# Centering and output projection of the product's groups as one matmul per token column on half of the array rows

## The chip, the cores and the metric

The kernel runs on one core of a Trainium2 chip. The metric is the device time of one execution in microseconds; the time of the kernel before is the median of three runs. A profile comes from one further execution, whose own time is given with it.

## The reference, cut to what matters

The input x is a 512 x 512 x 64 image in float32. Two layers follow each other. The first one normalises x by group, takes a layer norm over the 64 channels, makes gated left and right projections, multiplies them as a matrix product per channel over the image's axes, and finishes with a layer norm, a projection and a gate:

```
left  = (xn @ left_w + left_b) * mask * sigmoid(xn @ lgate_w + lgate_b)
right = (xn @ right_w + right_b) * mask * sigmoid(xn @ rgate_w + rgate_b)
out = einsum('bkjd,bkid->bijd', left, right)
out = _ln(out, onorm_w, onorm_b) @ out_w + out_b
x = x + out * sigmoid(xn @ ogate_w + ogate_b)
```

The second layer adds a spectral convolution with 12 x 12 modes of the group-normalised result. The change is in the line with `_ln(out)` and `out_w`: mean and variance of the product over its 64 channels, and the projection.

## The kernel before, in words

The mask leaves about half of the rows and columns, so the product is 256 x 256 tokens of 64 channels (`K` is 256). It is computed channel by channel and lies in SBUF as `places`, 128 partitions by 512 token columns of 64 channels. A *group* is 64 columns, so that there are 8 groups of the product (`first` = 8), followed by 32 units of x, each also 64 columns. One software pipeline runs over all of them (the loop over `s`): a step handles 8 columns, 128 partitions x 512 elements, and a group or a unit takes 8 steps (`SIZE`). The order of instructions is written out by hand (`manual_schedule`); every engine works through its own list in that order.

At step `s` the loop issues, for the groups of the product:

- TensorE transposes the 8 columns of step `s + 13` (`transpose`, L924): four 128 x 128 transposes, each of two columns, so that the channels of the one column lie on partitions 0 to 63 and those of the other on 64 to 127. ScalarE copies the result from PSUM to SBUF as `xt_c` (L927).
- TensorE multiplies the transposed columns of step `s` by `weights["out"]` (`times`, L934), a 128 x 128 matrix with the projection twice on its diagonal; the result is `w_ps`. The layer norm's centering and scale were multiplied into that matrix.
- TensorE multiplies the transposed columns of step `s + 12` by `center` (`centered`, L934), again a matrix of two diagonal blocks; the result `c_ps` is the columns less their means. ScalarE squares it into `sq_c` (L944).
- VectorE sums the squares of two steps over the channels (`summed`, L948), which are those of steps `s + 10` and `s + 11`. Once per group ScalarE takes the root of these sums (L954) and VectorE its reciprocal (L1106).
- VectorE multiplies `w_ps` by the reciprocal roots into `z_t` (L1112), and adds the bias for two steps at once (L1115). SyncE's queue stores `z_t` to DRAM as `u_d` (L1118), 512 KB per two steps.

The steps before 0 are the lead-in: transposes, centering, squares and sums, without `w_ps` and z. The steps of the last 13 before 64 already transpose and center the first units of x, whose matrices are `center_x` and `gate_x`.

Among the units the same steps go on with more work in them: ScalarE takes a sigmoid (L1068), POOL multiplies by rows of u that SyncE's queue loads from `u_d` (`load_u`, L965) or by the bias row (`gated`, L974) and adds to x (`added`, L978), VectorE takes statistics (L1023), and the result is stored. POOL's queue gathers x (`load`, L628). A closing stage, which is mostly transfers, adds the spectral part and writes the output.

An earlier stage, which makes the left and right sides, projects with matmuls on 64 of the 128 array rows: `project` (L746) multiplies `weights[k][h]` for each half `h` of the partitions and writes each half to its own bank of a tile of two banks.

PSUM in this stage: two tiles of one bank for the transposes, two for `c_ps`, two for `w_ps`, one bank for `scratch` (sums and biases), one for `f_ps`; all eight are taken.

Of the kernel before, what the change touches and what calls it, by code (L numbers as in the profile page):

```python
# [9 lines left out]
F32 = mybir.dt.float32  # L10
I32 = mybir.dt.int32
AF = mybir.ActivationFunctionType
ALU = mybir.AluOpType
AX = mybir.AxisListType
PSUM = bass.MemoryType.PSUM
DRAM = bass.MemoryType.DRAM

P = 128
N = 512
C = 64  # L20
# [26 lines left out]
def conv_preact_kernel(ctx: ExitStack, tc: tile.TileContext, t: dict):  # L47
    nc = tc.nc
    x, out = t["x"], t["out"]
# [18 lines left out]
    center = load_const("c_center", [P, P])  # L68
# [13 lines left out]
    with tc.tile_pool(name="ix", bufs=1) as xp, tc.tile_pool(  # L82
        name="ixp", bufs=1, space=PSUM
# [51 lines left out]
    weights, biases = {}, {}  # L135
# [476 lines left out]
    def compact(fc):  # L612
# [31 lines left out]
        with tc.tile_pool(name="xc", bufs=1) as cp:  # L644
            xc = cp.tile([P, K + 1, 2, C], F32, name="xc")
            with tc.tile_pool(name="f1", bufs=1) as sp, tc.tile_pool(name="f1x", bufs=2) as xp, tc.tile_pool(
                name="f1y", bufs=4
# [19 lines left out]
                for jc in range(NJ):  # L667
                    if jc % quarter == 0:
                        stats = sp.tile([P, 1, 16 * quarter, 6], F32, name="stats1c")
                    for r in range(4):  # L670
                        flat = xgs[jc][1][r].rearrange("p j c -> p (j c)")
                        for c in range(4):

                            ps = pt.tile([P, 4, P], F32, name="x_ps")
# [18 lines left out]
            with tc.tile_pool(name="fb", bufs=QB + 8) as gp, tc.tile_pool(name="fw", bufs=2) as wk, tc.tile_pool(  # L693
                name="fr", bufs=3
# [111 lines left out]
        with tc.tile_pool(name="tri", bufs=1) as trp:  # L806
# [50 lines left out]
            SIZE = 8  # L857
# [6 lines left out]
            with tc.manual_schedule(), tc.tile_pool(name="late", bufs=1) as lp:  # L864
# [27 lines left out]

                    (nc.gpsimd if h == 3 else nc.sync).dma_start(modes_t, modes_d[h * P : (h + 1) * P])

                with tc.tile_pool(name="np_x", bufs=LEAD + 2) as tp, tc.tile_pool(name="np_q", bufs=2) as sqp, tc.tile_pool(
                    name="np_s", bufs=3
                ) as small, tc.tile_pool(name="oz", bufs=4) as zp, tc.tile_pool(
                    name="o1", bufs=1
                ) as s1, tc.tile_pool(name="np_t", bufs=2, space=PSUM) as ps_t, tc.tile_pool(
                    name="np_c", bufs=2, space=PSUM  # L900
                ) as ps_c, tc.tile_pool(name="np_w", bufs=2, space=PSUM) as ps_w, tc.tile_pool(
                    name="np_n", bufs=1, space=PSUM
                ) as ps_n, tc.tile_pool(name="opf", bufs=1, space=PSUM) as ps_f:
                    scratch = ps_n.tile([P, 4, P], F32, name="scratch")
                    sum_ps = [scratch[:, 3, i * G : (i + 1) * G] for i in range(2)]
                    bias_ps = {"out": scratch[:, 2, :C], "ogate": scratch[:, 2, C:]}
# [11 lines left out]
                    def transpose(s):  # L918
                        k, n = divmod(s, SIZE)
                        flat = (place(k) if k < first else x_of(k - first)).rearrange("p n c -> p (n c)")  # L920
                        tps = ps_t.tile([P, 4, P], F32, name="t_ps")
                        for i in range(4):
                            o = (8 * n + 2 * i) * C
                            nc.tensor.transpose(tps[:, i, :], flat[:, o : o + P], ident)  # L924
                        xts[s] = tp.tile([P, 4, P], F32, name="xt_c")
                        if k < first:
                            nc.scalar.copy(xts[s], tps)  # L927
                        else:
                            nc.scalar.activation(xts[s], tps, AF.Identity, bias=ab1[:, 2:3])  # L929

                    def times(pool, name, s, w):
                        ps = pool.tile([P, 8, C], F32, name=name)
                        for i in range(4):
                            nc.tensor.matmul(ps[:, 2 * i : 2 * i + 2, :], xts[s][:, i, :], w, start=True, stop=True)  # L934
                        return ps

                    def centered(s):
                        return times(ps_c, "c_ps", s, center if s < first * SIZE else center_x)

                    def squared(s, cps):  # L940
                        n = s % SIZE
                        if n % 2 == 0:
                            sqs[s // 2] = sqp.tile([P, 16, C], F32, name="sq_c")
                        nc.scalar.activation(sqs[s // 2][:, 8 * (n % 2) : 8 * (n % 2) + 8, :], cps, AF.Square)  # L944

                    def summed(s):
                        k, n = divmod(s, SIZE)
# [99 lines left out]
                    for s in range(-LEAD, total_g + 2 * SIZE):  # L1047
# [6 lines left out]
                        if s + LEAD < total_g:  # L1054
                            transpose(s + LEAD)
                        wps = cps = None
                        if 0 <= s < total_g:
                            wps = times(ps_w, "w_ps", s, weights["out"] if k < first else gate_x)
                            del xts[s]
                        if 0 <= s + LEAD - 1 < total_g:  # L1060
                            cps = centered(s + LEAD - 1)
# [280 lines left out]
```

## Time and profile before

| what | value |
|---|---|
| median of 3 runs | 1892.95 us (1892.57 to 1894.03) |
| time of the profiled execution | 1886.98 us |
| its span, first to last instruction | 1885.2 us |
| PE busy in the span | 1683.2 us |
| DVE busy | 1458.5 us |
| ACT busy | 922.0 us |
| POOL busy | 873.0 us |
| first transposes of the product's groups | 666.3 us |
| z of step 0, of step 64 | 686.3 us, 829.1 us |
| end of the units | about 1546 us |

PE is TensorE's matmuls, PEld its weight loads, DVE is VectorE, ACT ScalarE, POOL GpSimd, SP SyncE. A float32 matmul of two operands is two records of the profile (two passes), a transpose is one. A matmul's record is longer than the time by which it moves the next one on, since matmuls are pipelined: what counts is the distance between starts. In a list of groups a line has the line of the kernel, engine, operation, output and inputs, sizes and count, then busy time, mean duration in ns, and the idle time of the engine before it with what ended it. In the waits a line has the waiting engine and tile, the one waited for, and the sum in us, the count and the longest wait.

### The profile page before, as it was taken

To read this page: it belongs to the slowest core of one execution; us is meant where nothing else is said; L and a number is where in the kernel's file an instruction comes from. 1 tells how busy PE (TensorE), PEld (TensorE's weight loads), DVE (VectorE), ACT (ScalarE), POOL (GpSimd) and SP (SyncE) were. 2 spreads that over 40 slices of the span, in tenths; PEclk is the share of its full clock that TensorE was granted. 3 is DMA by queue.
4 is the path that set the end of the run, shared out by engine and by line. 5 is a ranking of instruction groups with operands and counts; after the bars stand their busy time and mean duration, and the time that the engine had idled before them with its cause. 6 is when DMAs were issued, how large, how long until landed. Compare 5 with 4: busy or idle time off the path is not lost. (4 is left out here: it accounts for less than half of the span.)

```text
span 1885.2 us, 33737 instructions
## 1 busy us (share of the span) xinstructions
PE 1683.2 (89%) x11598; PEld 1350.9 (72%) x11598; DVE 1458.5 (77%) x2997; ACT 922.0 (49%) x1606; POOL 873.0 (46%) x678
## 2 busy tenths in 40 slices
PE   6779899998999999999999999999999956998873
PEld 5666666664788889998888888788888835664441
DVE  5989677777555568888999799979999994665552
ACT  3565555653222255567777677757767720111000
POOL 3655111111000000029999799979998982111110
PEclk9989899999999999999999899989999986555555
DMA  6999155556656534237777676767777589999999
GB/s 250 387 373 382 62 141 135 138 140 160 206 179 179 151 137 165 116 136 259 260 235 251 219 238 243 242 219 259 254 262 248 199 226 366 419 427 427 426 427 389
DMA packets 188868, 468.22 MB, mean 248 GB/s; under 512 B 35184, under 2 KB 134384, under 8 KB 147600
## 3 DMA queue, kind: packets, MB, share of 16 engines
q1 hardware_dynamic: 158192, 262.40, 41.4%
q0 software_dynamic: 27856, 202.19, 28.1%
q8 instruction: 94, 1.54, 0.3%
q10 hardware_dynamic: 2640, 1.38, 0.3%
q14 instruction: 86, 0.70, 0.1%
HBM read 278.13 MB, written 187.76 MB: 247 GB/s over the span
## 5 line engine op out<-in xcount | busy, mean ns | idle before, releaser
L934 PE MATMUL w_ps<-gate_x,xt_c 128*128 128x128 f32 x2048 | 281.9, 282 | 32.1 <-DVE z_t L1112 30.7
L978 POOL TENSOR_TENSOR places<-places,z_t 128x1024 f32<-128x1024 f32 x127 | 302.1, 2378 | 8.2
L934 PEld LDWEIGHTS w_ps<-gate_x,xt_c 128*128 128x128 f32 x2048 | 253.1, 195 | 49.1 <-DVE z_t L1112 48.6
L934 PE MATMUL c_ps<-center_x,xt_c 128*128 128x128 f32 x2048 | 276.3, 278 | 0.2
L934 PEld LDWEIGHTS c_ps<-center_x,xt_c 128*128 128x128 f32 x2048 | 252.5, 194 | 2.3 <-ACT xt_c L929 1.1
L944 ACT ACTIVATE sq_c<-c_ps 128x512 f32<-128x512 f32 x320 | 188.6, 590 | 104.3 <-PE c_ps L934 103.8
L1254 PE MATMUL l_ps<-places,rinv 24*128 24x512 f32 x512 | 209.7, 1128 | 31.7 <-DVE places L1261 25.7
L1112 DVE TENSOR_TENSOR z_t<-w_ps,rs_n 128x512 f32<-128x512 f32 x320 | 216.1, 675 | 23.0 <-PE w_ps L934 22.7
L1023 DVE BATCH_NORM_STATS2 stats2c<-places 128x6 f32<-128x128 f32 x1024 | 220.5, 279 | 8.1 <-POOL places L978 8.1
L948 DVE TENSOR_REDUCE scratch<-sq_c 128x16 f32<-128x1024 f32 x160 | 194.6, 1216 | 16.6 <-ACT sq_c L944 11.8
L1068 ACT ACTIVATE z_t<-z_t 128x1024 f32<-128x1024 f32 x128 | 135.5, 1058 | 142.0 <-DVE z_t L1115 117.7
L1115 DVE TENSOR_TENSOR z_t<-z_t,scratch 128x1024 f32<-128x1024 f32 x160 | 195.4, 1221 | 11.7 <-ACT rs_n L954 3.4
L1254 PEld LDWEIGHTS l_ps<-places,rinv 24*128 24x128 f32 x512 | 120.9, 304 | 115.4 <-DVE places L1261 73.1
L974 POOL TENSOR_TENSOR z_t<-z_t,bias_row_out 128x1024 f32<-128x1024 f32 x63 | 149.6, 2374 | 113.0 <-DMA places<-u_d 108.7
L924 PE MATMUL t_ps<-c_ident,places 128*128 128x128 f32 x1280 | 196.6, 277 | 1.3 <-DVE places L853 1.3
L1261 DVE TENSOR_TENSOR places<-places,l_ps 128x512 f32<-128x512 f32 x200 | 124.2, 683 | 86.5 <-DMA places<-x_h,dst_i 53.4
L929 ACT ACTIVATE xt_c<-t_ps,ab_xc 128x512 f32<-128x512 f32 x256 | 175.8, 687 | 23.8 <-PE t_ps L924 23.8
L924 PEld LDWEIGHTS t_ps<-c_ident,places 128*128 128x128 f32 x1280 | 148.9, 143 | 52.3 <-issue 52.3
L628 POOL DMA_INDIRECT places<-in_x,src_i x64 | 62.6, 978 | 261.9 <-PE c_ps L934 210.9
L974 POOL TENSOR_TENSOR z_t<-z_t,places 128x1024 f32<-128x1024 f32 x64 | 151.3, 2365 | 32.2 <-ACT z_t L1068 32.0
L678 DVE BATCH_NORM_STATS2 stats1c<-x_ps 128x6 f32<-128x512 f32 x256 | 156.0, 683 | 12.2 <-PE x_ps L677 11.3
L853 DVE SCALAR_TENSOR_TENSOR places<-tri_c_ps,slot_t,mask_s 128x256 f32<-128x256 f32 x128 | 73.1, 650 | 85.3 <-PE tri_c_ps L849 85.3
(203 smaller groups left out, 2641.9 us busy)
## 6 DMA issues: line engine op xcount, KB each, us to landing
x_h<-places SPq DMA_DIRECT2D x64, 1024.0 KB
out_x<-places SPq DMA_DIRECT2D x50, 1024.0 KB
places<-u_d SPq DMA_DIRECT2D x512, 64.0 KB
left_d<-o_c SPq DMA_DIRECT2D x64, 256.0 KB
right_d<-o_c SPq DMA_DIRECT2D x64, 256.0 KB
left_raw<-left_d SPq DMA_DIRECT2D x64, 256.0 KB
right_raw<-right_d SPq DMA_DIRECT2D x64, 256.0 KB
u_d<-z_t SPq DMA_DIRECT2D x32, 512.0 KB
```

The costliest lines, as they stand in the source:

```text
L678: nc.vector.bn_stats(stats[:, 0, 16 * (jc % quarter) + 4 * r + c, :], ps.rearrange("p i k -> p (i k)"))
L924: nc.tensor.transpose(tps[:, i, :], flat[:, o : o + P], ident)
L929: nc.scalar.activation(xts[s], tps, AF.Identity, bias=ab1[:, 2:3])
L934: nc.tensor.matmul(ps[:, 2 * i : 2 * i + 2, :], xts[s][:, i, :], w, start=True, stop=True)
L944: nc.scalar.activation(sqs[s // 2][:, 8 * (n % 2) : 8 * (n % 2) + 8, :], cps, AF.Square)
L948: nc.vector.tensor_reduce(totals[k % 2][:, 8 * (n - 1) : 8 * (n + 1)], sqs.pop(s // 2), AX.X, ALU.add)
L974: nc.gpsimd.tensor_mul(zs[k, c], zs[k, c], u)
L978: nc.gpsimd.tensor_add(xr, xr, zs.pop((k, c)))
L1023: nc.vector.bn_stats(st[k // 4][:, g, k % 4, :], x_of(k)[:, :, 2 * g : 2 * g + 2])
L1112: nc.vector.tensor_mul(z[:, 8 * odd : 8 * odd + 8, :], wps, rs)
L1115: nc.vector.tensor_add(z, z, bias.unsqueeze(1).to_broadcast([P, 16, C]))
L1254: nc.tensor.matmul(ps.rearrange("p j o -> p (j o)"), rinv[h, b, :], it[h], start=True, stop=True, tile_position=(32 * g, 0),)
```

## The change

For the groups of the product, the two matrices are put side by side: `both` has 64 columns of `center` and 64 columns of `weights["out"]`, once on partitions 0 to 63 and once on 64 to 127. `centered` multiplies the transposed columns by it, one half of the partitions at a time: eight matmuls with 64 rows per step, each for one token column and each 128 output columns wide. The results of the two halves go to the two banks of `y_ps` (two buffers, four banks). ScalarE squares the centered part as before and copies the projected part to SBUF, as the tile `xt_c` (15 buffers); the transposed columns lie in a tile of their own, `xt_y` (two buffers). `w_ps` is no longer computed for the groups: VectorE multiplies the copy by the reciprocal roots. When the pipeline reaches the first unit of x in `centered` (step 52), the pool of `y_ps` is closed and those of `c_ps` and `w_ps` are opened in its place. The units are computed as before.

```diff
--- before.py
+++ after.py
@@ -892,15 +892,24 @@
 
                     (nc.gpsimd if h == 3 else nc.sync).dma_start(modes_t, modes_d[h * P : (h + 1) * P])
 
-                with tc.tile_pool(name="np_x", bufs=LEAD + 2) as tp, tc.tile_pool(name="np_q", bufs=2) as sqp, tc.tile_pool(
+                with tc.tile_pool(name="np_x", bufs=LEAD + 2) as tp, tc.tile_pool(
+                    name="np_y", bufs=2
+                ) as yp, tc.tile_pool(name="np_q", bufs=2) as sqp, tc.tile_pool(
                     name="np_s", bufs=3
                 ) as small, tc.tile_pool(name="oz", bufs=4) as zp, tc.tile_pool(
                     name="o1", bufs=1
                 ) as s1, tc.tile_pool(name="np_t", bufs=2, space=PSUM) as ps_t, tc.tile_pool(
-                    name="np_c", bufs=2, space=PSUM
-                ) as ps_c, tc.tile_pool(name="np_w", bufs=2, space=PSUM) as ps_w, tc.tile_pool(
                     name="np_n", bufs=1, space=PSUM
-                ) as ps_n, tc.tile_pool(name="opf", bufs=1, space=PSUM) as ps_f:
+                ) as ps_n, tc.tile_pool(name="opf", bufs=1, space=PSUM) as ps_f, ExitStack() as products:
+
+                    ps_y = products.enter_context(tc.tile_pool(name="np_b", bufs=2, space=PSUM))
+                    ps_c = ps_w = None
+
+                    both = lp.tile([P, P], F32, name="both")
+                    for h in range(2):
+                        hs = slice(h * C, (h + 1) * C)
+                        nc.vector.tensor_copy(both[hs, :C], center[hs, hs])
+                        nc.vector.tensor_copy(both[hs, C:], weights["out"][hs, hs])
                     scratch = ps_n.tile([P, 4, P], F32, name="scratch")
                     sum_ps = [scratch[:, 3, i * G : (i + 1) * G] for i in range(2)]
                     bias_ps = {"out": scratch[:, 2, :C], "ogate": scratch[:, 2, C:]}
@@ -922,7 +931,7 @@
                         for i in range(4):
                             o = (8 * n + 2 * i) * C
                             nc.tensor.transpose(tps[:, i, :], flat[:, o : o + P], ident)
-                        xts[s] = tp.tile([P, 4, P], F32, name="xt_c")
+                        xts[s] = (yp if k < first else tp).tile([P, 4, P], F32, name="xt_y" if k < first else "xt_c")
                         if k < first:
                             nc.scalar.copy(xts[s], tps)
                         else:
@@ -935,13 +944,32 @@
                         return ps
 
                     def centered(s):
-                        return times(ps_c, "c_ps", s, center if s < first * SIZE else center_x)
+                        if s >= first * SIZE:
+                            return times(ps_c, "c_ps", s, center_x)
+
+                        ps = ps_y.tile([P, 2, 4, P], F32, name="y_ps")
+                        for i in range(4):
+                            for h in range(2):
+                                hs = slice(h * C, (h + 1) * C)
+                                nc.tensor.matmul(ps[:, h, i, :], xts[s][hs, i, :], both[hs], start=True, stop=True)
+
+                        xts[s] = tp.tile([P, 4, P], F32, name="xt_c")
+                        return ps
+
+                    def raw(s):
+                        return xts[s].rearrange("p i (h c) -> p (i h) c", h=2)
 
                     def squared(s, cps):
                         n = s % SIZE
                         if n % 2 == 0:
                             sqs[s // 2] = sqp.tile([P, 16, C], F32, name="sq_c")
-                        nc.scalar.activation(sqs[s // 2][:, 8 * (n % 2) : 8 * (n % 2) + 8, :], cps, AF.Square)
+                        sq = sqs[s // 2][:, 8 * (n % 2) : 8 * (n % 2) + 8, :]
+                        if s >= first * SIZE:
+                            nc.scalar.activation(sq, cps, AF.Square)
+                        else:
+                            by_half = lambda t: t.rearrange("p (i h) c -> p h i c", h=2)
+                            nc.scalar.activation(by_half(sq), cps[:, :, :, :C], AF.Square)
+                            nc.scalar.copy(by_half(raw(s)), cps[:, :, :, C:])
 
                     def summed(s):
                         k, n = divmod(s, SIZE)
@@ -1054,8 +1082,12 @@
                         if s + LEAD < total_g:
                             transpose(s + LEAD)
                         wps = cps = None
+                        if s + LEAD - 1 == first * SIZE:
+                            products.close()
+                            ps_c = products.enter_context(tc.tile_pool(name="np_c", bufs=2, space=PSUM))
+                            ps_w = products.enter_context(tc.tile_pool(name="np_w", bufs=2, space=PSUM))
                         if 0 <= s < total_g:
-                            wps = times(ps_w, "w_ps", s, weights["out"] if k < first else gate_x)
+                            wps = raw(s) if k < first else times(ps_w, "w_ps", s, gate_x)
                             del xts[s]
                         if 0 <= s + LEAD - 1 < total_g:
                             cps = centered(s + LEAD - 1)
```

## The prediction

> **What bounds the stage now.** I read the page's slices first, then the busy time by stretch, the waits inside the stretch, the order of time, and at last the older stage that already works on half the array rows. The product's groups run from about 666 us (first transposes) over step 0 at 686 us to step 64 at 829 us. Busy time by stretch (us of PE, PEld, DVE, ACT, POOL; then clock, DMA share, GB/s):
>
> ```profile
> 667.00:684.00 17.00, 15.97 (x142) 15.51 (x140) 6.07 (x6) 14.01 (x26) 2.92 (x3) 1.00 0.42 133
> 732.00:748.00 16.00, 16.00 (x146) 16.00 (x145) 13.62 (x16) 8.03 (x16) 0.00 (x0) 1.00 0.28 113
> 860.00:880.00 20.00, 18.22 (x158) 16.09 (x157) 19.49 (x45) 14.96 (x23) 19.60 (x9) 1.00 0.73 237
> ```
>
> In the steps (second line) TensorE never pauses and its clock is whole; DVE has 15% to spare, ACT half, DMA is at 28%. Later, among the units (third line), POOL and DVE are full instead. The waits between 690 and 826 us say the same: everyone waits for PE.
>
> ```profile
> ACT sq_c L944 <- PE c_ps L934: 67.3, 61, 1.2
> DVE z_t L1112 <- PE w_ps L934: 13.2, 23, 0.6
> ```
>
> In order of time (start, duration, engine, line), one step and a half:
>
> ```profile
> 739.05 1.23 DVE L948 TENSOR_REDUCE scratch<-sq_c 128x16 f32<-128x1024 f32 x1
> 739.92 0.60 PE L924 MATMUL t_ps<-c_ident,places 128*128 128x128 f32 x4
> 740.12 0.60 ACT L944 ACTIVATE sq_c<-c_ps 128x512 f32<-128x512 f32 x1 [1.15 <-PE c_ps L934]
> 740.18 0.68 DVE L1112 TENSOR_TENSOR z_t<-w_ps,rs_n 128x512 f32<-128x512 f32 x1
> 740.35 1.06 PE L934 MATMUL w_ps<-w_out,xt_c 128*128 128x128 f32 x8
> 740.61 0.58 ACT L927 COPY xt_c<-t_ps 128x512 f32<-128x512 f32 x1
> 741.25 1.06 PE L934 MATMUL c_ps<-c_center,xt_c 128*128 128x128 f32 x8
> 741.45 0.69 DVE L1112 TENSOR_TENSOR z_t<-w_ps,rs_n 128x512 f32<-128x512 f32 x1 [0.58 <-PE w_ps L934]
> 742.14 0.60 PE L924 MATMUL t_ps<-c_ident,places 128*128 128x128 f32 x4
> 742.17 1.22 DVE L1115 TENSOR_TENSOR z_t<-z_t,scratch 128x1024 f32<-128x1024 f32 x1
> 743.50 1.23 DVE L948 TENSOR_REDUCE scratch<-sq_c 128x16 f32<-128x1024 f32 x1
> ```
>
> Transposes follow each other every 742.14 - 739.92 = 2.22 us: 0.43 for four transposes, 0.90 for the eight passes of w_ps, 0.89 for those of c_ps (a float32 matmul is two records), that is 20 passes at 0.111. This is the period of a step, and PE sets it. (z at 829.12 less z at 686.30) / 64 = 2.23 agrees.
>
> The channel stage earlier shows two matmuls on 64 rows each, writing different halves of a two-bank tile:
>
> ```profile
> 350.06 0.19 PEld L746 LDWEIGHTS gates_c<-xnc,w_gates 64*128 64x128 f32 x2 [0.24 <-issue]
> 350.49 1.02 PE L746 MATMUL gates_c<-xnc,w_gates 64*128 64x512 f32 x4
> 351.45 0.66 PE L738 MATMUL rc_ps<-c_ident,rbc 128*128 128x128 f32 x4
> 352.38 1.06 PE L715 MATMUL cc_ps<-c_center,gc_t 128*128 128x128 f32 x8
> 353.36 1.13 PE L746 MATMUL sides_c<-xnc,w_sides 64*128 64x512 f32 x4
> L746 PE MATMUL gates_c<-xnc,w_gates x256: 589/589/693, 227.7 to 462.6; 64*128 64x512 f32 x128
> ```
>
> Four passes of 589 ns each (last line: min/median/max) fit in 1.02 us, so they ran two by two: 0.43 a pair. The two weight loads fit in 0.19, the length of one (182 to 187 ns), so loads of the two halves coincide as well.
>
> **What the Trainium skill says.** (1) TensorE: Matmul & The Clock Gate, "Part 3: Packing small matmuls — row/col tiling": matmuls and weight loads on different row groups run side by side. The gates' lines agree. (2) TensorEngine Tiling (Array Packing), "Key Properties": a change of tiling mode drains the array. The trace agrees. Into halves: cc_ps at 352.38 plus 8 x 0.111 hands over at 353.27; the first record of sides_c stands at 353.36 but is 693 instead of 589 ns long, so its stream began 0.10 later, at 353.46: 0.19 lost. Back: two pairs of gates_c end at 350.49 + 0.86 = 351.35, and the four transposes from 351.45 take 0.49 up to the next ones at 351.94 instead of 0.44: the stream began at 351.50, 0.15 lost. (3) The same page, "PSUM Bottleneck": tiling speeds up TensorE, not the emptying of PSUM. Here ACT gets one more copy for it. (4) VectorE: DVE Perf Modes, "Mode 2×_2P — use both read ports for one tensor": a float32 tensor_tensor stays at one element per cycle. In this trace a 128x512 reduction out of SBUF took 678 ns (L777) and z out of PSUM 675 (L1112), so z gains nothing by reading SBUF.
>
> **The change, part by part.** Steps 0 to 63 are meant, with a lead-in of 13 steps; squares run 12 steps ahead of z.
>
> 1. Removed: the four w_ps matmuls (8 passes) of each of the 64 steps, and the four c_ps matmuls on all rows, of which 64 steps too.
> 2. Added on PE: eight matmuls on 64 rows per step, 16 passes. As pairs they take 8 x 0.111 = 0.89. With transposes 0.44 and both changes of mode 0.34: **1.67 us** per step. No row of this trace shows 64-row passes of only 128 columns. Bounds: 0.89 if every pair overlaps; 1.78 if none does (then 2.56 per step). I take the first: the loads need 0.11 each and coincide by pairs (0.19 for two), and the 32-column loads of mixed_ps show 288 matmuls and 288 loads in 9.6 us, 17 ns per instruction, where this asks for 32 instructions in 0.89, 28 ns.
> 3. ACT: square and copy start 0.49 apart (740.12, 740.61). Three instead of two per step: 1.47, plus the root (0.31 per 8 steps) and waits of some 0.05: **1.56**. The square and the new copy read and write in runs of 64; no row shows that form. From 0.49 to the full 0.60 each: 1.56 to 1.9.
> 4. DVE: nothing is added or removed but PE's waits. Its own pace for two steps, start to start where nothing is waited for: reduction to z 1.13 (739.05, 740.18), z to the next instruction 0.60 (824.74 to 825.34 in the same list), z to bias sum 0.72 (741.45, 742.17), bias sum to reduction 1.33 (742.17, 743.50): 3.78. One reciprocal per eight steps adds 0.59 (825.34 to 825.93), 0.07 per step: **1.96**. This is the longest of the three: DVE becomes the bound, PE idles 15%.
> 5. The steps therefore take 64 x 1.96 = 125.6 instead of 142.8 us: 17.2 less.
> 6. The lead-in gets dearer. There DVE has only the reductions; PE's period is 1.33 now (c_ps at 674.54 and 675.87) and becomes 1.67: 12 x 0.34 = 4.1 more. ACT, at 1.56, stays below PE. The table load (1.28) and the first root stall PE by 0.66 in the middle now; with less slack in ACT it may be 1.2: 0.5 more.
> 7. The four 64x64 copies into both stand on DVE ahead of the last two instructions of L853, where DVE waits 1.53 us for PE (665.09 in the list): hidden by that wait; uncovered they'd cost about 4 x 0.2 = 0.8. The exchange of the PSUM pools at step 52 makes the first c_ps wait for ACT's last two reads of y_ps, about 1 us once; at that point PE has 0.3 us per step to spare and then 0.6 (no w_ps until step 64), so I count 0; uncovered 1.
> 8. Moved: the u_d stores (one per two steps on SP), the x loads on POOL's queue and the transposes that free their places keep their order. Stores come every 3.9 instead of 4.4 us, 512 KB each, some 133 GB/s, in a stretch whose DMA share is 28 to 71%. ACT's new copy waits for z of three steps before it (15 buffers); behind it stand the next transposes' copy and the squares, but the squares already lead DVE's reductions by one or two steps, so DVE doesn't wait.
>
> Sum: 17.2 - 4.1 - 0.5 = **12.6 us**, the place of z for step 64 going from 829.1 to 816.5. From there everything keeps its distance: POOL starts its chain with the first sigmoid (834.9 now) and is full from then on (8 operations of 2.37 and two loads of 0.98, 20.9 us per unit against a measured period of 21.0), its rows of u come from stores that move along, and the closing stage, where DMA is full, starts when the units are done. The profiled execution (span 1885.2, time 1886.98) would thus become 1872.6 in span. The median of the runs shown is 6.0 above the profiled time; I take the same 12.6 from it: 1892.95 - 12.6 = **1880.4 us**.
>
> **Rivals.**
> *The halves run one after the other* (slower). 2.56 per step on PE: lead-in 12 x (2.56 - 1.33) = 14.8, steps 0 to 51 52 x (2.56 - 2.23) = 17.2, steps 52 to 63 DVE-bound at 1.96, -3.2: +28.8, 1922 us. Against it stand the gates' lines; for it only that their passes are four times as long per load. It turns to a loss from a PE step of 2.11 on (12(p - 1.33) + 52(p - 2.23) = 3.2), that is when fewer than half of the pairs overlap.
> *ACT becomes the bound.* At 0.60 per instruction, with its waits, 1.9: still under DVE, so only the lead-in pays, 12 x 0.23 = 2.8: gain 9.8, 1883 us. It would have to exceed 0.63 each to slow the steps.
> *The gain is absorbed by the units.* If something that does not move set their start, the time would stay at 1893. The 108.7 us that POOL waits in the waits' list are put down to u_d, but what ended last is the first sigmoid (834.82), and u's rows are first read at 856.3, 24 us after their loads were issued. Little speaks for it.
>
> **How the numbers follow.** The forecast 0.74, ACT 0.10, absorbed 0.05, halves in turn 0.11. The forecast's own uncertainty is some 4 us: 64 steps at 1.93 to 2.00 and a lead-in 2 to 6 us dearer. With the rival of ACT and a part of overlap lost, the range is 1875 to 1889. About 0.2% (3.8 us) is what a measurement of this kernel can tell from no change: faster 0.83, same 0.06, slower 0.11.
>
> **What would show it.** Right: y_ps pairs with 16 passes in about 0.9 to 1.0 us; transposes 1.96 apart between step 0 and 52, 1.67 in the lead-in; in the waits of that stretch PE waiting for ACT or DVE and DVE waiting hardly for anything; DVE over 97% busy; z of step 64 near 816.5; the units' period unchanged at 21. Wrong: y_ps passes spread over 1.8 us, loads of the halves in turn, PE at 100% with DVE still waiting, a clock below 1.00 in that stretch, or POOL's first operation not earlier than 834.9.

## The result and the profile after

The changed kernel takes 1878.92 us (median of 4 runs, 1877.26 to 1882.64); the kernel before, measured beside it, takes 1893.49 (4 runs, the three of the table above among them, 1892.57 to 1894.11). The ratio is 0.9933, with a 95% interval of 0.9917 to 0.9948: faster by 14.6 us, or by 9.8 to 15.7 over the interval. The forecast was 1880.4, a gain of 12.6. The profiled execution took 1877.87 us, its span is 1876.0.

Busy time by stretch of the kernel after (us of PE, PEld, DVE, ACT, POOL; clock, DMA share, GB/s): the lead-in, 50 steps, a single stretch out of these, a part of that stretch, the stretch behind it, and one among the units.

```profile
667.00:684.00 17.00, 16.63 (x201) 13.79 (x201) 4.91 (x4) 14.85 (x29) 1.98 (x2) 1.00 0.35 125
692.00:790.00 98.00, 89.75 (x1019) 73.94 (x1020) 93.79 (x107) 81.00 (x161) 2.81 (x3) 0.97 0.43 168
722.00:738.00 16.00, 13.91 (x148) 11.42 (x144) 15.38 (x19) 11.60 (x24) 0.26 (x1) 0.89 0.54 208
732.00:735.30 3.30, 3.30 (x28) 2.74 (x25) 3.16 (x6) 2.60 (x5) 0.00 (x0) 0.50 0.39 159
738.00:754.00 16.00, 15.46 (x184) 12.68 (x184) 15.38 (x19) 14.34 (x30) 0.00 (x0) 1.00 0.35 142
860.00:880.00 20.00, 19.34 (x163) 16.75 (x162) 19.48 (x46) 15.62 (x24) 17.29 (x9) 1.00 0.91 336
```

In the lead-in TensorE is still full. In the steps DVE has become the full engine, and TensorE pauses for 8% of the time (89.75 of 98). The third and fifth lines show who leads: TensorE handled 148 matmul records in the one stretch and 184 in the next, DVE 19 instructions in both. The fourth line lies inside the third: for some 3.4 us TensorE was granted half its clock, and the 0.89 is the mean over the 16 us.

The waits of the steps, 692 to 790 us:

```profile
ACT rs_n L982 <- DVE scratch L976: 8.6, 5, 2.2
PEld y_ps L954 <- ACT xt_y L936: 8.5, 7, 2.3
...
ACT sq_c L971 <- PE y_ps L954: 2.4, 4, 0.9
...
DVE scratch L976 <- ACT xt_y L936: 0.5, 1, 0.5
```

DVE has one wait in this list, of 0.5 us. ACT's root, once in eight steps, waits for DVE's reductions, and TensorE then waits for ACT's copy of the transposed columns: one chain of waits that starts at DVE. Between these pauses TensorE goes on at its own pace. Before, ACT waited 67.3 us for TensorE.

In order of time, a step and a half of the kernel after (start, duration, engine, line):

```profile
740.25 1.23 DVE L976 TENSOR_REDUCE scratch<-sq_c 128x16 f32<-128x1024 f32 x1
...
741.02 0.60 ACT L971 ACTIVATE sq_c<-y_ps 128x512 f32<-128x512 f32 x1
741.39 1.28 DVE L1144 TENSOR_TENSOR z_t<-xt_c,rs_n 128x512 f32<-128x512 f32 x2
...
741.46 1.16 PE L954 MATMUL y_ps<-both,xt_y 64*128 64x128 f32 x16
741.52 0.58 ACT L972 COPY xt_c<-y_ps 128x512 f32<-128x512 f32 x1
741.98 0.60 ACT L936 COPY xt_y<-t_ps 128x512 f32<-128x512 f32 x1
...
742.56 0.65 PE L933 MATMUL t_ps<-c_ident,places 128*128 128x128 f32 x4
...
742.71 1.22 DVE L1147 TENSOR_TENSOR z_t<-z_t,scratch 128x1024 f32<-128x1024 f32 x1
...
743.14 1.16 PE L954 MATMUL y_ps<-both,xt_y 64*128 64x128 f32 x16
...
744.03 1.23 DVE L976 TENSOR_REDUCE scratch<-sq_c 128x16 f32<-128x1024 f32 x1
...
744.23 0.66 PE L933 MATMUL t_ps<-c_ident,places 128*128 128x128 f32 x4
```

TensorE's own period is 744.23 - 742.56 = 1.67, of which the sixteen passes, running two by two, have 742.56 - 741.46 = 1.10 with the way back to whole rows. DVE runs without a gap, two steps from 740.25 to 744.03 = 3.78, or 1.89, plus the reciprocal.

| place, us | before | after | forecast |
|---|---|---|---|
| first transposes of the groups | 666.4 | 666.7 | |
| lead-in, period of TensorE | 1.33 | 1.68 | 1.67 |
| z of step 0 | 686.3 | 690.5 | 690.9 |
| period of a step (mean of steps 10 to 45) | 2.22 | 1.95 | 1.96 |
| z of step 64 | 829.1 | 815.5 | 816.5 |
| POOL's first sum among the units | 834.9 | 819.2 | |
| last z | 1540.9 | 1529.4 | |

The gain is there at step 64 (13.6), and POOL starts its sums 15.7 us earlier. In this pair of profiles it shrinks to 11.5 at the last z and to 9.2 in the span. The code of the units is the same, and the time of one code varies: from step 64 to the last z the kernel after took 713.8 us in this profile and 721.7 in a second one (e9 below), the kernel before 711.8. The medians, 14.6 apart, show no such loss: the profiled execution of before lay 6.5 us under its median, that of after 1.1. So the stage, from the first transposes to the z of step 64, is what the experiments are judged by first: 162.7 us before, 148.8 after.

### The profile page after: what moved, and what is told of

The parts are those of the page before. It is cut to its first block, busy times and chain, and to the rows that moved or that the text cites. A ratio compares the mean times of both kernels' runs of the same rounds, so it can differ in the third digit from the quotient of the medians.

```text
span 1876.0 us, 33850 instructions
## 1 busy us (share of the span) xinstructions
PE 1653.0 (88%) x11598; PEld 1302.6 (69%) x11598; DVE 1454.2 (78%) x3001; ACT 953.8 (51%) x1670; POOL 873.8 (47%) x678
## 5 line engine op out<-in xcount | busy, mean ns | idle before, releaser
L976 DVE TENSOR_REDUCE scratch<-sq_c 128x16 f32<-128x1024 f32 x160 | 194.6, 1216 | 21.7 <-ACT sq_c L971 7.6
L1147 DVE TENSOR_TENSOR z_t<-z_t,scratch 128x1024 f32<-128x1024 f32 x160 | 195.4, 1221 | 11.3 <-ACT rs_n L982 3.3
L933 PE MATMUL t_ps<-c_ident,places 128*128 128x128 f32 x1280 | 201.4, 281 | 1.3 <-DVE places L853 1.3
L1144 DVE TENSOR_TENSOR z_t<-w_ps,rs_n 128x512 f32<-128x512 f32 x256 | 171.9, 672 | 7.4 <-PE w_ps L943 7.4
L1002 POOL TENSOR_TENSOR z_t<-z_t,places 128x1024 f32<-128x1024 f32 x64 | 151.5, 2367 | 35.9 <-ACT z_t L1100 35.7
L968 ACT ACTIVATE sq_c<-c_ps 128x512 f32<-128x512 f32 x256 | 150.7, 589 | 31.4 <-PE c_ps L943 31.1
L663 ACT COPY xc<-xg 128x128 f32 x352 | 105.0, 298 | 67.5 <-POOL xc L663 43.5
```

Source lines behind the costliest of these rows:

```text
L968: nc.scalar.activation(sq, cps, AF.Square)
L976: nc.vector.tensor_reduce(totals[k % 2][:, 8 * (n - 1) : 8 * (n + 1)], sqs.pop(s // 2), AX.X, ALU.add)
L1002: nc.gpsimd.tensor_mul(zs[k, c], zs[k, c], u)
L1144: nc.vector.tensor_mul(z[:, 8 * odd : 8 * odd + 8, :], wps, rs)
L1147: nc.vector.tensor_add(z, z, bias.unsqueeze(1).to_broadcast([P, 16, C]))
```

## The experiments

The theory: the half rows shorten TensorE's step because the two halves run at once; DVE's own work then sets the step; and what the stage gains, the run gains. The rivals: that the halves' side-by-side run isn't the source, that another engine than DVE is the bound, and that the units absorb a gain. Periods are means from transpose to transpose, in the lead-in without its first two steps and at steps 10 to 45; "one" is a single run.

| kernel | lead-in / step, us | stage, us | time, us | before beside it | ratio (95%) |
|---|---|---|---|---|---|
| before | 1.33 / 2.22 | 162.7 | | | |
| after | 1.68 / 1.95 | 148.8 | 1878.92 | 1893.49 | 0.9933 (0.9917 to 0.9948) |
| e1 halves in turn | 2.23 / 2.23 | 169.5 | 1898.67 | 1890.36 | 1.0045 (1.0028 to 1.0061) |
| e2 all rows | 2.17 / 2.17 | 166.1 | 1893.99 | 1890.36 | 1.001 (0.9996 to 1.0025) |
| e3 no bias sum | 1.68 / 1.68 | 128.0 | 1854.45 | 1890.36 | 0.9807 (0.9779 to 0.9836) |
| e4 bias sum on POOL | 1.68 / 1.86 | 145.1 | 1872.91 | 1890.36 | 0.9896 (0.9865 to 0.9928) |
| e5 after, POOL busy | 1.68 / 2.27 | 167.4 | 1893.46 (one) | 1886.45 | |
| e6 before, POOL busy | 1.33 / 2.22 | 162.8 | 1883.96 (one) | 1886.45 | |
| e7 scale on POOL | 1.68 / 1.68 | 130.3 | 1853.51 | 1886.45 | 0.9833 (0.9798 to 0.9868) |
| e8 two steps at once | 1.62 / 1.65 | 129.2 | 1856.88 | 1886.45 | 0.9842 (0.9809 to 0.9874) |
| e9 after, again | 1.68 / 1.96 | 149.0 | 1880.99 | 1895.26 | 0.9921 (0.9889 to 0.9952) |
| e10 e7, again | 1.68 / 1.69 | 132.2 | 1860.61 | 1895.26 | 0.9808 (0.9776 to 0.984) |

### The halves in turn

```diff
-                        for i in range(4):
-                            for h in range(2):
-                                hs = slice(h * C, (h + 1) * C)
+                        for h in range(2):
+                            hs = slice(h * C, (h + 1) * C)
+                            for i in range(4):
                                 nc.tensor.matmul(ps[:, h, i, :], xts[s][hs, i, :], both[hs], start=True, stop=True)
```

> The eight 64-row matmuls of a step in another order: the four of the upper half first, then the four of the lower half, nothing else. Theory (the gain rests on the two halves running side by side, pair by pair): the 16 passes then take about 15 or 16 slots of 0.111 us instead of 8, a step of PE 1.67 + 0.8 = 2.45 to 2.56 us, above DVE's 1.95; z of step 64 about 40 us later than after the change, the time about 1915 to 1922 us, slower than before the change. Rival (PE needs no neighbours in order, it reorders or the gain is only from what waits in SBUF): step 1.95, time unchanged at 1879.

It took 1898.67 us, 8.3 more than before. In order of time, TensorE alone:

```profile
742.69 1.71 PE L954 MATMUL y_ps<-both,xt_y 64*128 64x128 f32 x16
744.33 0.66 PE L933 MATMUL t_ps<-c_ident,places 128*128 128x128 f32 x4
744.91 1.71 PE L954 MATMUL y_ps<-both,xt_y 64*128 64x128 f32 x16
```

The same sixteen passes now spread over 1.71 instead of 1.16 us, and the step is 744.91 - 742.69 = 2.22. So the direction is that of the theory, and the size is not: with 0.44 for the transposes and 0.34 for the two changes of mode, 1.44 is left, 13 times 0.111, where 16 were expected and the alternating order has 8. The starts of the single passes show why: while the upper half's later passes still followed each other, at 745.461 and 745.573, a further pass stood beside them at 745.467, with its weight load at 745.466, and two more pairs follow. A record doesn't name its half, but by these distances TensorE let the second half begin three passes early. That the step equals the one of before is chance; the loss is the lead-in's, whose period went from 1.33 to 2.23.

### One matmul per pair of columns on all rows

Everything else of the change is kept: the third copy on ACT, the projected values in SBUF, the pools.

```diff
-                    both = lp.tile([P, P], F32, name="both")
...
+                    both = lp.tile([P, 2, P], F32, name="both")
+                    nc.vector.tensor_copy(both[:, 0], center)
+                    nc.vector.tensor_copy(both[:, 1], weights["out"])
...
-                                nc.tensor.matmul(ps[:, h, i, :], xts[s][hs, i, :], both[hs], start=True, stop=True)
+                            nc.tensor.matmul(ps[:, i], xts[s][:, i, :], both, start=True, stop=True)
```

> Centering and projection in one matmul per pair of token columns on all 128 rows (two diagonal blocks side by side, 256 output columns), the projected values waiting in SBUF as in the change. Four matmuls per step instead of eight, no change of tiling mode. Theory (streamed columns count, not instructions or waits): 8 passes of 256 columns at 0.213 = 1.71 plus four transposes 0.44, PE step 2.15 us; lead-in 12 x (2.15 - 1.33) = +9.8, steps 0 to 51 -4, steps 52 to 63 -3, in sum about +2 against before the change: 1893 to 1898. Rival (the gain came from VectorE no longer waiting for w_ps, or from the eight matmuls less per step): the time of the change, 1879.

As expected: 1893.99 us, which can't be told from before. In order of time, TensorE alone:

```profile
741.11 0.60 PE L931 MATMUL t_ps<-c_ident,places 128*128 128x128 f32 x4
741.54 1.89 PE L950 MATMUL y_ps<-both,xt_y 128*128 128x256 f32 x8
743.27 0.60 PE L931 MATMUL t_ps<-c_ident,places 128*128 128x128 f32 x4
```

A step is 743.27 - 741.11 = 2.16, and 743.27 - 741.54 = 1.73 is for eight passes of 256 columns, 0.216 each: twice the columns take nearly twice the time, and no more than some 0.06 per step comes with half as many matmuls and weight loads. The rest of the change without the half rows is thus worth a shorter step by 0.06, eaten up by the dearer lead-in (12 x 0.84 = 10). The whole gain of the change comes from halves that run at once.

### Without the bias sum

DVE's sum of the bias to z is left out for the groups, so this kernel doesn't compute the bias of the product.

```diff
-                                nc.vector.tensor_add(z, z, bias.unsqueeze(1).to_broadcast([P, 16, C]))
+                                if k >= first:
+                                    nc.vector.tensor_add(z, z, bias.unsqueeze(1).to_broadcast([P, 16, C]))
```

> The change with the bias sum of the product's groups left out (L1147 for the groups; the bias is missing from u). Theory (VectorE sets the step after the change, PE is next at 1.67): VectorE's step falls from 1.95 to about 1.3, PE's 1.67 sets steps 0 to 51, about 1.35 steps 52 to 63: 52 x 0.28 + 12 x 0.6 = 22 us less than after the change, about 1857. Rival (ScalarE already sets it together with VectorE at 1.9, or PE does): 1874 to 1879.

1854.45 us. A stretch of 80 us (columns as above):

```profile
690.00:770.00 80.00, 80.00 (x958) 66.28 (x954) 59.99 (x78) 75.22 (x150) 1.87 (x2) 1.00 0.51 198
```

and its waits:

```profile
DVE scratch L976 <- ACT sq_c L971: 20.0, 24, 1.0
```

With DVE's 1.22 us per two steps gone, DVE is busy for 60 of 80 us and waits, TensorE is full again, at its own 1.68, and the stage is 20.8 us shorter than after's. Hence DVE was the bound and TensorE, not ACT, is next. The run fell by 35.9 us against before, the stage by 34.7: nothing was absorbed.

### The bias sum on POOL

The gathers of x on POOL's queue are put to earlier steps, so that the sums don't queue behind their waits.

```diff
-                        if 0 <= v + 3 < len(units):
+                        if s in (-4, 4, 20):
+                            for r in range(2):
+                                load((-4, 4, 20).index(s), r)
+                        if 3 <= v + 3 < len(units):
...
-                                nc.vector.tensor_add(z, z, bias.unsqueeze(1).to_broadcast([P, 16, C]))
+                                if k < first:
+                                    nc.gpsimd.tensor_add(z, z, rows_of["out"].unsqueeze(1).to_broadcast([P, 16, C]))
+                                else:
+                                    nc.vector.tensor_add(z, z, bias.unsqueeze(1).to_broadcast([P, 16, C]))
```

> The change with the bias sum of the product's groups moved from VectorE to POOL (128x1024, 2.37 us per two steps), and the gathers of the first three units of x placed in POOL's order at steps -4, 4 and 20, where their places come free, so that they don't stand behind these sums. Theory: as with the bias left out, since POOL needs only 1.19 us per step: 18 to 22 us less than after the change, 1857 to 1861. Rival (POOL and VectorE slow each other down, or POOL is late for the first unit because of its sums): half of that or less, 1868 or more.

It missed the theory's time: 1872.91, in the rival's range, and a step of 1.86 in place of 1.68. In order of time, the longest case:

```profile
727.93 3.37 DVE L1147 TENSOR_TENSOR z_t<-xt_c,rs_n 128x512 f32<-128x512 f32 x1
...
728.37 2.37 POOL L1151 TENSOR_TENSOR z_t<-z_t,bias_row_out 128x1024 f32<-128x1024 f32 x1
```

DVE's z begins first and lasts 3.37 us, until 0.56 us after the end of POOL's sum (731.30 against 730.74). As a rule the first z of two steps begins some 0.92 us into POOL's sum and takes about 2.0 us, again until 0.55 us after its end, and the second takes 0.68. Over all z of 690 to 785 us (min/median/max in ns):

```profile
L1147 DVE TENSOR_TENSOR z_t<-xt_c,rs_n x50: 621/861/3368, 690.3 to 783.9; 128x512 f32<-128x512 f32 x50
```

In the kernel after it is

```profile
L1144 DVE TENSOR_TENSOR z_t<-xt_c,rs_n x50: 626/681/685, 690.5 to 785.0; 128x512 f32<-128x512 f32 x50
```

So this z slows down when POOL works beside it. Both its inputs lie in SBUF; the change moved one of them there from PSUM, and the next two kernels ask whether that matters.

### POOL kept busy, after and before

Both kernels get four idle sums on POOL for every two steps, which nothing uses (and the gathers as above).

```diff
+                    idle = lp.tile([P, 4, C], F32, name="idle")
+                    nc.gpsimd.memset(idle, 0.0)
...
                                 if k < first:
+                                    for _ in range(4):
+                                        nc.gpsimd.tensor_add(idle, idle, rows_of["out"].unsqueeze(1).to_broadcast([P, 4, C]))
```

> The change with idle work on POOL in the product's groups: four sums of 128x256 per two steps into a tile that nobody uses (about 0.6 us each), the first gathers of x placed as in the version with the bias on POOL. Theory (z, with both inputs in SBUF since the change[...]): z of the groups, 0.68 us alone, takes 0.9 to 1.3 us on the mean in the stretch where POOL works, and the steps there take 2.2 us or more instead of 1.95. Rival (the long z of the version with the bias on POOL were waits for POOL's data or for z's buffers): z stays at 0.68 and the steps at 1.95.

> The same idle work on POOL in the kernel before, where z reads w_ps from PSUM. Theory: z keeps 0.68 us and the steps 2.22 us, since only one of its inputs is in SBUF. Rival: z is longer here too where POOL works.

All z of 690 to 785 us, first in the kernel after with a busy POOL, where the second line is DVE's sum of the bias:

```profile
L1149 DVE TENSOR_TENSOR z_t<-xt_c,rs_n x42: 680/1063/1221, 691.3 to 784.6; 128x512 f32<-128x512 f32 x42
L1152 DVE TENSOR_TENSOR z_t<-z_t,scratch x21: 1220/1221/1223, 688.8 to 781.1; 128x1024 f32<-128x1024 f32 x21
```

and in the kernel before with a busy POOL:

```profile
L1117 DVE TENSOR_TENSOR z_t<-w_ps,rs_n x44: 629/682/694, 690.3 to 785.0; 128x512 f32<-128x512 f32 x44
```

Out of SBUF the median z goes from 681 to 1063 ns, the step from 1.95 to 2.27 and the stage from 148.8 to 167.4 us; out of PSUM nothing moves (682 ns, 2.22, 162.8 us). Within the first run the bias sum, which reads z from SBUF and the bias from PSUM, keeps its 1221 ns too. POOL's idle sums, first in the kernel after, then in the kernel before:

```profile
L1155 POOL TENSOR_TENSOR idle<-idle,bias_row_out x128: 721/732/1110, 676.6 to 806.8; 128x256 f32<-128x256 f32 x128
```

```profile
L1123 POOL TENSOR_TENSOR idle<-idle,bias_row_out x128: 722/728/746, 672.0 to 791.1; 128x256 f32<-128x256 f32 x128
```

Beside z out of SBUF some of them are stretched to 1.1 us, beside z out of PSUM none. The Trainium skill says so in "SBUF — State Buffer", section "Who interferes with whom": a DVE instruction with two inputs in SBUF contends with a GpSimd instruction that reads SBUF, one with at most one does not, and whoever issues first blocks the other. These lines agree on the first two points. On the third they agree in part. The blocking goes both ways: in the first of these kernels a z that began at 727.62, with 0.08 us of an idle sum to go, kept its 0.68 us, and POOL's next sum, begun 0.16 us behind it, took 1.11. But the order of the recorded starts doesn't always tell who will wait: with the bias sum on POOL, a z that began 0.02 us ahead of POOL's sum took 2.94 us, and the one of 3.37 us began 0.44 us ahead, though POOL was then already at a gather (727.41 to 728.35). In the change itself POOL is busy for 2.8 of 98 us of the steps, so next to none of this price is paid there.

### The scaling on POOL

Here POOL takes z instead (1.04 us each), and DVE adds the bias out of PSUM one step later; the gathers of x are placed as with the bias sum on POOL.

```diff
+                        if waiting is not None and n % 2 == 0:
+                            zb, j = waiting
+                            waiting = None
+                            nc.vector.tensor_add(zb, zb, bias_ps["out"].unsqueeze(1).to_broadcast([P, 16, C]))
+                            nc.sync.dma_start(
+                                u_d[:, j : j + 8].rearrange("p j r c -> p (j r c)"), zb.rearrange("p n c -> p (n c)")
+                            )
...
-                            nc.vector.tensor_mul(z[:, 8 * odd : 8 * odd + 8, :], wps, rs)
...
+                            on = nc.gpsimd if k < first else nc.vector
+                            on.tensor_mul(z[:, 8 * odd : 8 * odd + 8, :], wps, rs)
+                            if odd and k < first:
+                                waiting = z, JC * k + 8 * c
```

> The change with the product of the waiting values and the reciprocal roots (z) on POOL, and the bias sum on VectorE one step later, behind the next reduction; the first gathers of x placed at steps -4, 4 and 20. Everything is computed. Theory: VectorE keeps the reduction (one input) and the bias sum (one input in SBUF, one in PSUM)[...]; its step is about 1.3 us, POOL's about 1.2, so PE's 1.67 sets steps 0 to 51: as with the bias left out, 20 to 22 us less than after the change, 1855 to 1860. Rival (reductions and sums are slowed by POOL as well, or POOL needs more than 1.67 us per step): 1866 or more.

1853.51 us. A stretch of 75 us (columns as above):

```profile
690.00:765.00 75.00, 75.00 (x896) 62.11 (x896) 57.13 (x51) 70.90 (x141) 46.36 (x47) 1.00 0.55 210
```

and z and the bias sum in it (min/median/max in ns):

```profile
L1156 POOL TENSOR_TENSOR z_t<-xt_c,rs_n x59: 1035/1042/1054, 689.5 to 784.1; 128x512 f32<-128x512 f32 x59
...
L1144 DVE TENSOR_TENSOR z_t<-z_t,scratch x29: 1220/1222/1222, 692.0 to 784.3; 128x1024 f32<-128x1024 f32 x29
```

Each of DVE's remaining instructions has at most one input in SBUF, and neither engine is stretched. TensorE is full at 1.68 per step. With the bias computed, this version takes 32.9 us less than the kernel before on its chip, where leaving the bias out (e3) took 35.9 less on another: it beats both kernels.

### Two steps' transposes together

On top of the last kernel, the changes of mode are halved: two steps' transposes, then two steps' half-row matmuls.

```diff
-                        if s + LEAD < total_g:
+                        edge = first * SIZE - LEAD - 1
+                        paired = -LEAD < s <= edge
+                        if paired and s % 2 == 0:
+                            transpose(s + LEAD)
+                            if s < edge:
+                                transpose(s + LEAD + 1)
+                        elif not paired and s + LEAD < total_g:
                             transpose(s + LEAD)
...
+                        if paired and s % 2 == 0:
+                            both_ps = [centered(s + LEAD - 1), centered(s + LEAD)]
```

> The former version with the groups' steps taken two by two on TensorE: transposes of two steps, then the matmuls of two steps, so that the tiling mode changes half as often. Theory (a change there and back costs 0.34 us, and PE sets the step in the former version): PE 1.50 per step; ScalarE, at 1.5 to 1.56, is as long: 0.11 to 0.17 less per step over 64 steps of lead-in and steps, 7 to 11 us less than the former version, about 1847 to 1852. Rival (the drain is hidden, or ScalarE already holds at 1.67): no difference from the former version.

In order of time:

```profile
730.92 1.09 PE L933 MATMUL t_ps<-c_ident,places 128*128 128x128 f32 x8
...
733.20 0.59 ACT L936 COPY xt_y<-t_ps 128x512 f32<-128x512 f32 x1 [0.42 <-PE y_ps L954]
...
733.93 1.09 PE L933 MATMUL t_ps<-c_ident,places 128*128 128x128 f32 x8
```

Here two steps take 733.93 - 730.92 = 3.01 on TensorE instead of 3.36, as hoped. But only every second pair of steps does: the others take 3.46 to 3.68, so that a step takes 1.65 on the mean, not 1.5. The stretch, and two of its waits:

```profile
690.00:765.00 75.00, 71.62 (x910) 62.72 (x908) 57.52 (x52) 69.94 (x145) 47.75 (x48) 1.00 0.56 212
```

```profile
ACT xt_y L936 <- PE y_ps L954: 5.1, 11, 0.5
PE y_ps L954 <- ACT xt_y L936: 3.4, 12, 0.4
```

TensorE is no longer full. It waits for ACT's copy into `xt_y`, and ACT waits for TensorE to free one of the two tiles of `xt_y` (the 0.42 in the second line above). 1856.88 us is no gain over e7's 1853.51; the expected 7 to 11 us did not come. ACT is busy for 69.94 of 75 us, close to full, but since the two engines wait for each other, the runs don't show whether ACT's own pace or the two tiles set the 1.65. A third tile of `xt_y` wasn't tried.

### The change and the best version on one chip

> The changed kernel once more, on the chip of the next run and beside the kernel before. Theory: stage from the first transposes to z of step 64 148.8 us as in its first profile, 13.9 less than before the change; time 12 to 15 us below the kernel before of the same chip, ratio 0.992 to 0.994. Rival (a part of that difference was the chip or the hour): less than 8 us.

> The version with z on POOL once more, beside the changed kernel. Theory: its stage is 18.5 us shorter than the change's (130.3), and the time follows one to one: 17 to 20 us below the changed kernel. Rival (the units give a part back): 12 or less.

1880.99 us for the change (14.3 under before) and 1860.61 for the scaling on POOL, 20.4 less again. By the earlier pairs these would be 14.6 and 18.3, so the order of the three kernels is settled. The second one's stage is 132.2 us instead of 130.3: TensorE had half its clock in the first steps of the lead-in, which came to step 0 some 1.6 us later than in e7 (23.2 against 21.7 us after the first transposes).

## Why the prediction was right

The time (1878.92 for 1880.4) and its reason hold: TensorE's step got shorter by the halves' running at once, DVE set the pace instead, and the run gained what the stage gained. By the steps of the prediction's sum:

1. and 2. TensorE's step: forecast 1.67, measured 1.68 in the lead-in, where TensorE is full. The passes start 0.112 us apart two by two, and what is left, 1.68 less 0.44 and 0.90, is 0.34 for both changes of mode; e8, which saves one change there and back in two steps, has 3.36 - 3.01 = 0.35. The bound without overlap (2.56) was also the price of the rival, and there 2.23 was measured: its 16 passes in turn were mis-sized, 13 slots.
3. ACT's 1.56 was never the bound in the change, and the runs of 64 cost nothing: the square took 597 ns and the new copy 580 in the median. Where ACT came closest to being the bound, in e8, a step takes 1.65.
4. and 5. DVE's pace: 3.78 for two steps in the forecast and in the lines above; 1.95 per step measured for 1.96. From z of step 0 to z of step 64 it is 125.0 us (forecast 125.6, before 142.8). TensorE's pauses, put at 15% of the time, are 8% in the records; the two spells of half clock, in which its work takes longer, are a part of the difference.
6. The lead-in: from the first transposes to z of step 0 it took 23.8 instead of 19.9 us, 3.9 more; forecast 4.6. The half microsecond for the table load and the root hardly showed: TensorE's pause there grew from 0.66 to 0.80 us, not to 1.2.
7. The four copies ran at 663.8 to 664.1 us, ahead of an instruction of DVE that waited for TensorE until 665.4: hidden. The exchange of pools held TensorE's first `c_ps` for 0.6 us, at 787.3, and shows no stall in the place of step 64.
8. What comes after keeps its distance. Against the kernel before, the stage and the time move together: after -13.9 and -14.6, e1 +6.8 and +8.3, e2 +3.4 and +3.6, e3 -34.7 and -35.9, e4 -17.6 and -17.5, e7 -32.4 and -32.9, e9 -13.7 and -14.3. In two cases they differ by 4 us, once each way: e8 -33.5 and -29.6, e10 -30.5 and -34.7. (The single runs of e5 and e6 have +4.7 and +7.0, +0.1 and -2.5.) So gains and losses of the stage reach the end, and the rival of the absorbing units is out. The units' period was read too low, 21.0: from POOL's first sum of a unit to that of the next it is 21.4 in most units of both profiles, and unchanged as forecast.

The formula of the rival with the halves in turn can be put to the test with e1 and e2, whose steps are known: 12(p - 1.33) + 52(p - 2.22) - 3.2 gives +8 for p = 2.23 and +4 for 2.17; the stages show +6.8 and +3.4. So the turning point of 2.11 is good to a few hundredths.

Three of the signs were ill chosen. DVE was to be over 97% busy and is at 95.7% (93.79 of 98): of the 4.2 us that are missing one wait takes 0.5, and the rest are gaps of some 0.03 or 0.10 us between its instructions. Transposes were to stand 1.96 apart; they do so on the mean only, because TensorE works through most steps in 1.68 and then pauses. And a clock below 1.00 was to mean trouble. It was halved twice in the steps, from 731.9 to 735.3 and from 762.6 to 766.0 us, and TensorE's sixteen passes then spread over 1.78 us (at 731.52) instead of 1.16; but DVE was busy for 3.16 of the 3.30 us in the stretch shown, as elsewhere, so nothing was lost. The sign should have asked whether DVE waits.

The exact match owes something to luck as well: 12.6 was derived for one profile and the medians gave 14.6, and the kernel before, from which it was subtracted, has medians from 1886.45 to 1895.26 in the later pairs.

## What to carry to other kernels

When a change lightens the bound engine, work out the period of every other engine from start to start, since the gain is the way to the second longest one and not what was taken away; the lead-in, where the old second engine has nothing to do, may even get dearer. Matmuls on half the rows pay when the two halves alternate in the program, and their changes of mode belong into the sum. Before an operand is moved from PSUM to SBUF, look at what POOL does beside the instruction that reads it: here the same z cost 0.68 us or more than 1, with nothing changed in it.

## What the runs showed of the hardware

- Half-row passes of 128 columns run in pairs 0.112 us apart when the halves alternate. With one half after the other about three passes still overlap (13 slots of 0.111 instead of 16).
- Going to half rows and back cost 0.34 us together, as what is left of a step of 1.68, and 0.35 by the pairs of steps in e8.
- A z of 128x512 with both inputs in SBUF took 0.68 us beside an idle POOL, 1.06 in the median beside a busy one, and up to 3.37; with one input in PSUM it stayed at 0.68. POOL's sums of 128x256 took up to 1.11 us beside the first and at most 0.75 beside the second.
- TensorE's granted clock was halved for 3.4 us at a time. In the steps of the kernel after this came twice (from 731.9 and from 762.6 us), each time at the end of a pause of TensorE of 2.09 us, and not after its other pauses there, of up to 1.60; e9 shows the same. But e5 has a pause of 3.07 us (from 768.4) without it, and in e10 it came (from 669.3) after one of 1.31 us that the other runs have too. In the stretches of e3 and e7, where TensorE was full, the clock was 1.00. The cause wasn't tested.
